# Normalising the first five tiles of a graph layer in one batch, with the input and the first weights on one DMA queue

## The chip, the cores and the metric

The kernel runs on one core of one Trainium2 chip. The metric is the device time of one execution in microseconds (us), as the median of several runs. Five engines work side by side, each in the order of its own instruction list: TensorE (PE, with its weight loads listed as PEld), VectorE (DVE), ScalarE (ACT), GpSimd (POOL) and SyncE (SP). SP, ACT and POOL also issue DMAs, each on a queue of its own. Engines wait for each other by semaphores.

## The reference

One layer of a graph transformer on 3125 nodes with 256 channels and 53125 edges sorted by target:

```python
xn = _layernorm(x, axis=-1)
x = x + _L0_gnn_ref(xn, src, dst, edge_weight, gnn_W, gnn_b) + _L0_mix_ref(xn[None], ...)[0]
x = x + _L0_ffn_ref(_layernorm(x, axis=-1)[None], gate_w, gate_b, w1, w2, w3)[0]

def _L0_gnn_ref(x, edge_row, edge_col, edge_val, W, b):
    msgs = edge_val[:, None] * x[edge_col]
    agg = jax.ops.segment_sum(msgs, edge_row, num_segments=N_NODES)
    return jnp.einsum('nf,of->no', agg, W) + b
```

`_L0_mix_ref` is a linear attention with 8 heads: keys and queries pass elu + 1, and the sum over all nodes of K^T V is needed before any output. Two layer norms and a two-layer network follow. `_L0_ffn_ref` is a mixture of 16 experts with two chosen for each node. Everything that this text is about happens before the sum K^T V is complete.

## The kernel before

The 3125 nodes are held as 25 tiles of 125 rows, in `x_all` (partition, tile, channel). The opening loops over the tiles, `for t in range(NT)`, and does three things for each:

- `normed(t)`: DVE writes `xn = (x - mean) * rstd` (line 417), PE turns it with two transposes into `tok` (L429), ACT copies it to `xnT` (L430). Tile t + 1 is normed before tile t is projected.
- `projected(t)`: PE multiplies by the three joined weights `wcat`: node transform and keys into `big` (L438), values into `tok` (L440). ACT makes `ek` and `k_sb` (L442, L444), the copy `y` (L449) and `v_sb` (L448). DVE joins `ek` and `k_sb` to the key (L446). SP stores `y` (L450), after which it may issue a later load (`load_later`: the x tiles 15 to 19 after tile 0, 20 to 24 after tile 1).
- `summed(t - 1)`: PE adds K^T V of the tile before to `pkv` (L462). It reads `k_sb`, so it waits for the DVE step of L446. PE's list in the opening is thus tok(t+1), big(t), values(t), pkv(t-1), over and over.

The mean and the variance of a tile come from `bn_stats` (L104) and `bn_aggr` (L105) on DVE. The reciprocal square root is worked out on DVE, for a batch of tiles at once, by `rsqrt` (L92 to L99): four small instructions and three rounds of three, 13 in all, each of which needs the one before. `BATCHES` says which tiles share one such chain, and `AHEAD` after which `normed(t)` the moments of which tiles are taken. `factors` (L391, L392) adds two small instructions for each batch.

```python
LOADS = ((0, 2), (2, 5), (5, 10), (10, 15), (15, 20), (20, 25))
BATCHES = ((0, 2), (2, 5), (5, 12), (12, 25))
AHEAD = {1: (2, 5), 2: (5, 9), 3: (9, 12), 4: (12, 15), 6: (15, 17), 9: (17, 21), 10: (21, 25)}
```

`LOADS` says in which pieces x is loaded. The first two pieces are issued at once on SP's queue, the third and fourth when the moments of the first batch have been found.

Beside this, `windows()` prepares the edges, in pieces that are called by `LISTS` after certain tiles. DVE makes `heads` from the first target of each row of edges, PE turns it into a row (`ph`, L244) after a run of matmuls on ones, `busy(16)` (L240), which do no useful work. DVE counts with `cmp_h` (L249) and a reduction (L251), and gets five columns `row_i` (L254). POOL gathers `rows` with them by five indirect DMAs (L258). For each of these, DVE compares (`cmp_r`, L268), reduces (L269) and works out `start_i` (L270 to L273), with which POOL gathers `win` (L274). From `win` DVE makes keys (L287 to L302), after which PE, ACT and POOL build `keys` and `wgts`. They are needed from tile 18 (`HOT`), where the adjacency matrices begin (L336 to L360).

The instructions of each engine are put in order by a scheduler when the kernel is built: pieces of different chains lie between each other on DVE, and each engine keeps that order strictly.

Of the kernel before, what the change touches and what calls it, by code (L numbers as in the profile page):

```python
# [18 lines left out]
C = 256  # L19
# [31 lines left out]
ATT_EPS = 1e-6  # L51
LN_EPS = 1e-5
LOADS = ((0, 2), (2, 5), (5, 10), (10, 15), (15, 20), (20, 25))
BATCHES = ((0, 2), (2, 5), (5, 12), (12, 25))

LISTS = {1: 1, 6: 1, 7: 2, 8: 2, 14: 1, 15: 1, 16: 1}
AHEAD = {1: (2, 5), 2: (5, 9), 3: (9, 12), 4: (12, 15), 6: (15, 17), 9: (17, 21), 10: (21, 25)}
HOT = 18
GROUP = 4

# [2 lines left out]
def tile_gps_layer(ctx: ExitStack, tc: tile.TileContext, a: dict, out: bass.AP):  # L63
    nc = tc.nc
# [37 lines left out]
    def stats(mv, src):  # L102
        st = small.tile([P, 6], F32, name="bn_st")[: src.shape[0]]
        nc.vector.bn_stats(st, src)  # L104
        return nc.vector.bn_aggr(mv, st)  # L105
# [55 lines left out]
    def load_x(queue, t0, t1):  # L161
        return queue.dma_start(x_all[:, t0:t1, :], a["x"][:, t0:t1, :])

    wcat = w_mix.tile([128, 2, 3 * C], F32, name="wcat")
    load_x(nc.sync, *LOADS[0])
    nc.scalar.dma_start(dst_0, a["dst"].rearrange("(p j) -> p j", p=V)[:, 0:1])
    for i, name in enumerate(("gnn_WT", "Wk", "Wv")):
        nc.scalar.dma_start(wcat[:, :, i * C : (i + 1) * C], a[name].rearrange("(k p) o -> p k o", p=128))
    load_x(nc.sync, *LOADS[1])
    wq = w_mix.tile([128, 2, C], F32, name="wq")  # L170
    wm = w_mix.tile([128, 2, C], F32, name="wm")
    w1 = w_mix.tile([128, 4, F], F32, name="w1")
# [47 lines left out]
    def bank_a(of=4 * P):  # L220
        return adj_ps.tile([128, 512], F32, name="pa")[:, :of].rearrange("p (i e) -> p i e", e=of // 4)
# [8 lines left out]
    def windows():  # L230
# [6 lines left out]
        def busy(n):  # L237
            pd = bank_a()
            for i in range(n):
                nc.tensor.matmul(pd[:, i % 4, :], lhsT=ones, rhs=ones, start=True, stop=True)  # L240

        busy(16)
        ph = bank_a()[:V, 0, :V]
        nc.tensor.matmul(ph, lhsT=ones[:V, :V], rhs=heads, start=True, stop=True)  # L244
        yield ins
# [148 lines left out]
    def moments(t0, t1):  # L394

        for i in range(t0, t1):
            found = stats(mv[:, i, :], x_all[:, i, :])
        for t0, end in BATCHES:
            if end == t1:
                ready[t0] = rsqrt(mv[:, t0:t1, 1], t1 - t0)  # L400
        return found

    pieces = windows()
    with tc.issue_after(next(pieces).ins):
        found = moments(*BATCHES[0])

# [3 lines left out]
    def normed(t):  # L410

        nonlocal rstd, r0
        for t0, t1 in BATCHES:
            if t == t0:
# [4 lines left out]
        with tc.issue_after(ins.ins):  # L419
            for batch in BATCHES:  # L420
                if t == batch[0]:
                    factors(*batch, rstd)
            for _ in range(LISTS.get(t, 0)):
                next(pieces, None)
            if t in AHEAD:
                moments(*AHEAD[t])
        ptr = a_ps.tile([128, 2, P], F32, name="tok", bufs=3)
# [259 lines left out]
    for g, (nt, n_adj, n_early) in enumerate(groups):  # L687
# [5 lines left out]
        i = 0  # L693
# [599 lines left out]
```

## Time and profile before

| | |
|---|---|
| median of 3 runs | 1035.18 us (1035.09 to 1035.54) |
| the profiled execution: its time, its span | 1034.76 us, 1033.0 us |
| PE busy | 1004.1 us, 97% of the span |
| DVE busy | 654.8 us, 63% |
| ACT, POOL busy | 263.1 us, 215.7 us |
| mean granted TensorE clock | 0.997 |
| DVE busy in 5 to 10, 10 to 15, 15 to 20, 20 to 25, 25 to 30 us | 4.48, 4.75, 5.00, 4.59, 5.00 us of 5 each |

The times in the profile count from the start of the span. A row of the timeline has the start, the time from the first start to the last end, the engine, the line of the kernel, the operation, the tiles that it writes and reads, and how many instructions are merged; in brackets stands the idle time before it and what ended it. A float32 matmul is listed as two records of PE.

### The profile page before, as it was taken

The numbers are of one execution on the slowest core, as the hardware profiler recorded it, in microseconds if no ns is written. First come the engines' busy times: TensorE is split into PE (matmuls) and PEld (weight loads), VectorE is DVE, ScalarE is ACT, GpSimd is POOL, SyncE is SP. The second block draws the span as 40 slices with busy tenths as digits, with TensorE's granted clock in tenths as the row PEclk, the third lists the DMA queues.
The fourth block names the chain that finished last, engine by engine and source line by source line (L and its number), as shares of the span: only waits on it lengthen the run. The fifth ranks groups of instructions, "written<-read, shape, count | busy, mean of one in ns | idle before, by whom it ended". The sixth has DMA issues, their size and how long they took to land.

```text
span 1033.0 us, 16284 instructions
## 1 busy us (share of the span) xinstructions
PE 1004.1 (97%) x6006; PEld 804.3 (78%) x6006; DVE 654.8 (63%) x1750; ACT 263.1 (25%) x577; POOL 215.7 (21%) x200
## 2 busy tenths in 40 slices
PE   8999999999999999999999999999999999999995
PEld 5667666686786877878877888887888888888884
DVE  8878699889887897956598148786932222222221
ACT  3666423323223133222131000003111111111110
POOL 3420101023100000000000001114535444545432
PEclk9999999999999999999999999999999999999998
DMA  6444104344343444544454446565757757667662
GB/s 216 93 135 140 52 34 174 127 135 138 124 137 137 140 159 142 179 164 143 153 184 155 154 159 172 184 193 180 225 141 222 244 173 228 201 201 226 205 191 26
DMA packets 70024, 165.01 MB, mean 160 GB/s; under 512 B 10816, under 2 KB 29584, under 8 KB 65964
## 3 DMA queue, kind: packets, MB, share of 16 engines
q1 hardware_dynamic: 53466, 138.02, 39.3%
q0 software_dynamic: 15520, 25.04, 10.7%
q8 instruction: 50, 0.82, 0.3%
q10 hardware_dynamic: 946, 0.79, 0.2%
q14 instruction: 42, 0.34, 0.1%
HBM read 105.85 MB, written 57.93 MB: 159 GB/s over the span
## 4 chain that ended last, share of the span: by engine, by line
PE 70%; DVE 11%; issue 2%; ACT 0%; POOL 0%; POOLq 0%; ACTq 0%; DVEq 0%
PE ph L1002 17%; PE pb L626 13%; PE po L1028 10%; PE po L739 8%; PE pa L356 6%; PE big L663 5%; PE tok L674 3%; DVE wone L341 2%; PE pa L626 1%; PE ptr L988 1%; PE big L478 1%; DVE one L336 1%; DVE wone L351 1%; PE ph L800 1%; PE big L490 1%
## 5 line engine op out<-in xcount | busy, mean ns | idle before, releaser
L1002 PE MATMUL ph<-xTb,wt 128*128 128x256 f32 (+2 forms) x992 | 204.5, 355 | 0.8 <-issue 0.8
L1002 PEld LDWEIGHTS ph<-xTb,wt 128*128 128x128 f32 x992 | 171.5, 190 | 24.8 <-ACT xTb L991 4.7
L626 PE MATMUL pb<-y_early,nbr 125*125 125x256 f32 x736 | 170.6, 382 | 0.4 <-DVE x_all L628 0.4
L341 DVE TENSOR_TENSOR wone<-one,wgts 128x1536 bf16<-128x1536 bf16 x150 | 141.1, 953 | 25.5 <-PE pa L356 25.3
L626 PEld LDWEIGHTS pb<-y_early,nbr 125*125 125x125 f32 x736 | 133.7, 188 | 18.6 <-DVE x_all L628 1.0
L356 PEld LDWEIGHTS <-one 128*128 128x128 bf16 x1875 | 117.3, 97 | 39.1 <-issue 18.8
L359 ACT COPY adj<-pa 128x512 f32<-128x512 f32 (+1 forms) x157 | 91.8, 586 | 195.5 <-PE pa L356 169.4
L356 PE MATMUL pa<-wone,one 128*128 128x128 bf16 x1875 | 130.5, 219 | 2.1 <-DVE wone L341 0.9
L1009 DVE TENSOR_TENSOR hid<-hid,ph 128x512 f32<-128x512 f32 (+2 forms) x62 | 38.3, 618 | 145.7 <-PE ph L1002 136.9
L1028 PE MATMUL po<-wt,hid 128*128 128x256 f32 (+1 forms) x456 | 115.2, 385 | 0.8 <-DVE yb L1031 0.7
L739 PE MATMUL po<-y_late,nbr 125*125 125x256 f32 x450 | 102.3, 381 | 0.5 <-DVE x_all L628 0.5
L336 DVE TENSOR_TENSOR one<-iota,keys 128x1024 bf16<-128x1024 bf16 x150 | 101.1, 695 | 0.6 <-POOL wgts L318 0.6
L1032 POOL DMA_INDIRECT out<-yb,to_l x45 | 70.9, 1576 | 114.6 <-DMA out<-yb,to_l 51.0
L1028 PEld LDWEIGHTS po<-wt,hid 128*128 128x128 f32 (+1 forms) x456 | 79.2, 184 | 17.6 <-DVE yb L1031 5.6
L739 PEld LDWEIGHTS po<-y_late,nbr 125*125 125x125 f32 x450 | 82.4, 188 | 12.1 <-DVE x_all L628 0.9
L1008 ACT ACTIVATE hid<-ph 128x512 f32<-128x512 f32 (+2 forms) x62 | 33.6, 542 | 208.5 <-PE ph L1002 202.5
L1031 DVE TENSOR_SCALAR yb<-po,sh 128x256 f32<-128x256 f32 (+1 forms) x57 | 27.5, 482 | 57.3 <-PE po L1028 55.2
L752 POOL IOTA rev<- 125x16 f32 x1 | 0.2, 154 | 295.4 <-PE pb L626 295.4
L701 POOL TENSOR_TENSOR x_all<-x_all,cb 128x256 f32<-128x256 f32 x25 | 25.7, 1050 | 147.0 <-DVE x_all L628 139.4
L628 DVE TENSOR_TENSOR x_all<-x_all,pb 125x512 f32<-125x512 f32 (+1 forms) x37 | 24.3, 658 | 41.7 <-PE pb L626 41.7
L663 PE MATMUL big<-xnT,w 128*128 128x500 f32 (+1 forms) x112 | 48.8, 548 | 0.0
L674 PE MATMUL tok<-w,hT 128*125 128x256 f32 x200 | 47.9, 383 | 0.0
(285 smaller groups left out, 1197.8 us busy)
## 6 DMA issues: line engine op xcount, KB each, us to landing
wt<-in_w SPq DMA_DIRECT2D x28, 1536.0 KB
adj_d<-adj SPq DMA_DIRECT2D x156, 256.0 KB
nbr<-adj_d SPq DMA_DIRECT2D x25, 576.0 KB
nbr<-adj_d SPq DMA_DIRECT2D x50, 256.0 KB
nbr<-adj_d SPq DMA_DIRECT2D x25, 512.0 KB
wt<-in_w POOLq DMA_DIRECT2D x3, 1536.0 KB
out<-x_all SPq DMA_DIRECT2D x25, 125.0 KB
x_all<-in_x SPq DMA_DIRECT2D x4, 640.0 KB
```

The costliest lines, as they stand in the source:

```text
L336: nc.vector.tensor_tensor(one.rearrange("p b h e j -> p (b h) e j"), iota_2[:, None, :, :].to_broadcast(shape), ql.rearrange("p b h j -> p ...
L341: nc.vector.tensor_tensor(wone, one[:, :, 1:2, :, :].to_broadcast(shape), w[:, :, :, None, :].to_broadcast(shape), op=ALU.mult)
L356: nc.tensor.matmul(pa[:, j, :], lhsT=one[:, j // 2, 0, :, j % 2], rhs=wone[:, j // 2, i, :, j % 2], start=(i == 0), stop=(i == 2))
L359: copied = nc.scalar.copy(rows[:, :n, :], pa[:, :n, :])
L626: nc.tensor.matmul(pb[:V, i, :], lhsT=rows[:V, k - t0, :V], rhs=y_of(k)[:V], start=(k == t0 and i == 0), stop=(k == t1 - 1), skip_group_ch ...
L663: nc.tensor.matmul(ph[:, :w], lhsT=w1[:, k, j * 128 : (j + 1) * 128], rhs=rhs, start=(k == 0), stop=(k == 3))
L674: nc.tensor.matmul(po, lhsT=hT[:, j, i * V : (i + 1) * V], rhs=w2[:, j, :], start=(j == 0), stop=(j == 3))
L739: last = nc.tensor.matmul(pg, lhsT=rows[:V, k - t0, :V], rhs=y_of(k)[:V], start=(k == t0), stop=(k == t1 - 1))
L1002: last = nc.tensor.matmul(p[:, m, :w], lhsT=self.wt[:, i, k * F + at : k * F + at + 128], rhs=self.xT[:, k, :w], start=(k == 0), stop=(k = ...
L1009: self.units = nc.vector.tensor_tensor(hid, hid, pre[1], op=ALU.mult)
L1028: last = nc.tensor.matmul(po[:n_r, r, :], lhsT=self.hid[:, k, r * LANES : r * LANES + n_r], rhs=self.wt[:, 2, k * C : (k + 1) * C], start= ...
L1032: made.append(nc.gpsimd.indirect_dma_start(out=out[:, :], out_offset=bass.IndirectOffsetOnAxis(ap=at, axis=0), in_=yb[:n_r, r, :], in_offs ...
```

## The change

Four things are changed. The first batch has five tiles in place of two, so that the batches are 5, 4, 6 and 10 tiles in place of 2, 3, 7 and 13. The later moments are taken in other portions and after other tiles. The three pieces of `wcat` are issued on SP's queue behind both first pieces of x, where they were issued on ACT's queue. And `busy(16)` becomes `busy(24)`.

```diff
-BATCHES = ((0, 2), (2, 5), (5, 12), (12, 25))
+BATCHES = ((0, 5), (5, 9), (9, 15), (15, 25))
...
-AHEAD = {1: (2, 5), 2: (5, 9), 3: (9, 12), 4: (12, 15), 6: (15, 17), 9: (17, 21), 10: (21, 25)}
+AHEAD = {2: (5, 7), 3: (7, 9), 4: (9, 12), 5: (12, 15), 9: (15, 18), 10: (18, 21), 11: (21, 25)}
...
     load_x(nc.sync, *LOADS[0])
     nc.scalar.dma_start(dst_0, a["dst"].rearrange("(p j) -> p j", p=V)[:, 0:1])
+    load_x(nc.sync, *LOADS[1])
     for i, name in enumerate(("gnn_WT", "Wk", "Wv")):
-        nc.scalar.dma_start(wcat[:, :, i * C : (i + 1) * C], a[name].rearrange("(k p) o -> p k o", p=128))
-    load_x(nc.sync, *LOADS[1])
+        nc.sync.dma_start(wcat[:, :, i * C : (i + 1) * C], a[name].rearrange("(k p) o -> p k o", p=128))
...
-        busy(16)
+        busy(24)
```

The order of the instructions, as built: PE's is the same but for the eight more matmuls, POOL's is the same, ACT loses its three DMA issues, SP gains them behind the second piece of x and has the small store `first_d` (L283) two stores of `y` earlier. On DVE the order differs in the first 180 or so of some 1,870 rows, up to the keys of the edges, and is the same from there to the end.

## The prediction

> **What bounds the kernel now.** First the engines' busy time in the page: PE is busy nearly all the time, so the end is set by PE's idle time and by useless work on it.
>
> ```profile
> PE 1004.1 (97%) x6006; PEld 804.3 (78%) x6006; DVE 654.8 (63%) x1750; ACT 263.1 (25%) x577; POOL 215.7 (21%) x200
> ```
>
> Then the waits of PE in the first 140 us (waiting tile and line, what released it, us in total, times, longest):
>
> ```profile
> PE tok L429 <- DVE less L392: 2.6, 1, 2.6
> PE pa L240 <- POOL ones L134: 1.9, 1, 1.9
> PE tok L429 <- DVE xn L417: 0.4, 1, 0.4
> PE pkv L462 <- DVE k_sb L446: 0.3, 1, 0.3
> ```
>
> The largest wait is one of 2.6 us for a normed tile. The timeline of the opening shows where it comes from (start, time taken, engine, line):
>
> ```profile
> 4.11 0.74 DVE L104 BATCH_NORM_STATS2 bn_st<-x_all 128x6 f32<-128x256 f32 x2
> ...
> 5.11 0.17 DVE L92 TENSOR_SCALAR rs_v<-mv 128x2 f32<-128x2 f32 x1
> ...
> 7.55 0.41 DVE L417 TENSOR_SCALAR xn<-x_all,mv,rs_y 128x256 f32<-128x256 f32 x1
> ...
> 8.34 0.74 DVE L104 BATCH_NORM_STATS2 bn_st<-x_all 128x6 f32<-128x256 f32 x2
> ...
> 9.73 0.17 DVE L92 TENSOR_SCALAR rs_v<-mv 128x3 f32<-128x3 f32 x1
> ...
> 12.18 0.17 DVE L254 CAST row_i<-row_f 125x5 int32<-125x5 f32 x1
> ...
> 12.69 1.41 POOL L258 DMA_INDIRECT rows<-in_dst,row_i  x1 [9.30 <-DVE rs_s L98]
> ...
> 13.50 0.69 DVE L417 TENSOR_SCALAR xn<-x_all,mv,rs_y 128x256 f32<-128x256 f32 x1
> ...
> 14.33 0.41 PE L429 MATMUL tok<-ident,xn 125*128 125x125 f32 x2 [2.58 <-DVE less L392]
> ...
> 15.38 0.38 DVE L446 SCALAR_TENSOR_TENSOR k_sb<-ek,k_sb 125x256 f32<-125x256 f32 x1
> ```
>
> The first chain runs from 4.11 to 7.55. The second, for tiles 2 to 4, starts only then, is mixed with the edges' counting, and gives xn at 13.50. PE, done with tiles 0 and 1 at 11.76, waits to 14.33. From there PE's own steps set the pace, 3.24 us a tile:
>
> ```profile
> 17.16 0.61 PE L462 MATMUL pkv<-v_sb,k_sb 125*128 125x129 f32 x4
> 20.40 0.61 PE L462 MATMUL pkv<-v_sb,k_sb 125*128 125x129 f32 x4
> ...
> 26.89 0.61 PE L462 MATMUL pkv<-v_sb,k_sb 125*128 125x129 f32 x4
> ...
> 47.23 0.68 PE L462 MATMUL pkv<-v_sb,k_sb 125*128 125x129 f32 x4 [0.32 <-DVE k_sb L446]
> ...
> 60.59 0.61 PE L462 MATMUL pkv<-v_sb,k_sb 125*128 125x129 f32 x4
> ```
>
> These are pkv(0), (1), (3), (9) and (13). I use them as posts: whatever the change does has happened by pkv(13), since from there on all five engines have their old order and edge work follows PE. From 26.89 to 60.59 are 33.70 us, where ten steps take 32.43: small waits for L446 cost 1.27 us there. DVE, 63% busy on average, is 90 to 100% busy from 5 to 30 us.
>
> **The first chain** grows by three tiles. Two take 1.00 us from 4.11 to 5.11, three take 1.39 from 8.34 to 9.73: 0.39 a tile, 1.17 in all. The 13 steps of rsqrt stay 2.44 us (5.11 to 7.55), and a five-column operand in place of two costs nothing (0.17 us with 2 and with 13 columns). So xn(0) starts at 8.72, and PE, 0.47 us behind as before, turns it at 9.19, not at 8.02. The batches are four before and after, so no chain is saved in number.
>
> **busy(24)** adds 16 records. The run's records come about 0.21 us apart at first, 0.11 at its end (32 take 5.3 us in all; 11 touch the last full microsecond, 7 the second). At 0.11 it ends 1.8 us later, near 8.9, and `ph` before 9.2: hidden, by xn(0). Without that cover it would cost 1.8 us, at 0.21 3.4. [...]
>
> **One queue.** x and `wcat` ahead of tile 0 are 0.66 + 0.79 MB. Even at the 190 GB/s of the first 5 us, from a start near 2.0, all has landed by 9.6; at the 308 GB/s of the next 5 us, before 7. The first `big` needs it at 10.1 (8.91 + 1.17). I take nothing, and at most 0.3 for the third x piece, which is issued 1.2 us later. SP waits nowhere else for the change; `first_d` sits two stores of y earlier, and nobody in the opening waits for a y store.
>
> **The wait removed** is 2.58. If only PE counted, pkv(0) would move from 17.16 to 15.76 (+1.17 - 2.58 = -1.40). But pkv(0) reads k_sb(0), and in the changed order DVE does all of this from xn(0) to L446 of tile 0: five xn, seven stats with their aggregates, cmp_h, the reduction, row_i and 12 of the 13 steps of the second rsqrt. Against the list before (7.83 us, from 7.55 to 15.38) that is two xn more (0.33 each), one stats (0.33) and two aggregates (0.085 each), less two of by/less (0.07) and one step (0.19): +0.83. L446 then starts at 8.72 + 8.66 = 17.4. Adding up the new list by its steps from start to start, with six steps of rsqrt hidden, gives 16.8. I take 17.1. With its 0.40 and 0.15 to PE, pkv(0) comes at 17.65: **+0.5** (0.2 to 0.8). PE's wait of 2.58 becomes one of 1.9 in front of pkv(0).
>
> **Tiles 1 to 3.** row_i falls 5.6 to 5.9 us behind xn(0), at 14.3 to 14.6, not 12.18, and the first gather is issued 0.5 later: 14.9, not 12.69. Up to 17.8 gathers moved 0.30 MB, and one is 0.21 MB, so the first landed near 17.5, 4.8 after its issue; it will land at 19.7 or later. In the changed order the first cmp_r stands ahead of k_sb(1), where before two more k_sb were ahead of it. With 20.2 for the landing k_sb(1) starts at 20.75: pkv(1) at 21.3, **+0.9**. Between k_sb(1) and k_sb(3) DVE has four cmp_r (0.51), three reductions (0.50), two xn and two k_sb (0.33 each) and 22 small ones (0.07 to 0.08 hidden): 6.6 to 6.9. Beside them POOL's gathers stretch an instruction now and then: xn took 0.69 during the first gather, 0.41 otherwise. I add 0.3. k_sb(3) starts at 27.8 and pkv(3) at 28.35, **+1.5** (0.6 to 2.5).
>
> [...]
>
> **What comes back.** Before, the cmp_r work and the late `win` gathers pressed on k_sb(4) to k_sb(11), which is the 1.27. In the changed order the last start_i stands ahead of k_sb(4), near 30 in place of 32.85, so `win` lands earlier and DVE is ahead from there. I take 1.1 of it back. Sum: +1.5 - 1.1 = **+0.4**. The profiled time of 1034.76 becomes 1035.2; the median lies 0.42 above the profiled one, so 1035.6. Bounds: -0.65 with pkv(3) at 27.5 and all 1.27 back; +2.0 with pkv(3) at 28.9 to 29.4 and only half of it back. With 0.3 for a median's spread that is 1034.2 to 1037.3.
>
> **Rivals.** (a) DVE keeps up, and PE alone counts: -1.4, and -2.7 if the 1.27 goes as well. For it: the wait of 2.58 is real and PE has nothing else to wait for. Against: DVE's list ahead of L446, which would have to be 1.9 us shorter.
> (b) The first gather lands late. At 20.6 to 22.0 the gathers moved 0.04 MB beside 0.37 MB of an x load: the load held the fourth up by some 1.4 us. Now that load comes up to 1.4 us earlier and the gathers 2.2 later, so it may meet the first. Each us past 20.2 moves k_sb(1) by one and isn't given back: at 21.9 the whole is +2.1, at 22.5 +2.7. Against: the first gathers came through beside the load before it.
> (c) The waits only change names, and the total is within 0.2 us: the forecast's lower half.
>
> **How the numbers follow.** 0.2% is 2.07 us, about what a measurement of this kernel can tell from no change. Forecast with (c), 0.72: within it but for 0.03 slower. (a), 0.14: within it at -1.4, and 0.04 below it. (b), 0.14: 0.10 slower, the rest within. So faster 0.04, same 0.83, slower 0.13.
>
> **What would show it.** Right: no wait of tok L429 near 12, a wait of 1.5 to 2.5 us of pkv L462 on k_sb, xn(0) at 8.7, pkv(0) at 17.4 to 18.0, pkv(3) late by 1 to 2 us, pkv(9) no longer waiting, pkv(13) near 61.0. Wrong: pkv(0) before 16.5 (rival a), pkv(1) past 22.5 (b), `big` waiting for `wcat`, or a difference that arises after 61 us.

## The result, and the profile after

The changed kernel takes 1038.05 us in the median of ten runs (1037.22 to 1039.52), the kernel before 1035.14 (ten runs). The ratio is 1.0027 (95% interval 1.0018 to 1.0036): slower by 2.9 us. The forecast was 1035.6, with a range to 1037.3. The profiled execution took 1038.04 us, its span is 1036.3 us, 3.3 more than before.

The busy line of the page hardly differs: PE has 16 more records.

```profile
PE 1007.6 (97%) x6022; PEld 807.2 (78%) x6022; DVE 652.5 (63%) x1750; ACT 263.4 (25%) x577; POOL 216.4 (21%) x200
```

The waits of PE in the first 140 us of the changed kernel (waiting tile and line, releaser, us in total, times, longest):

```profile
PE pkv L462 <- DVE rs_v L92: 1.9, 1, 1.9
...
PE pkv L462 <- DVE rs_y L99: 0.7, 1, 0.7
```

The wait of `tok` (L429) is gone, and two waits of `pkv` stand in its place. The releaser's name is that of the DVE instruction nearest in time: `pkv` reads `k_sb`, which DVE ends just then. The timeline of the changed kernel shows the opening:

```profile
4.24 0.75 DVE L104 BATCH_NORM_STATS2 bn_st<-x_all 128x6 f32<-128x256 f32 x2
...
6.41 0.17 DVE L92 TENSOR_SCALAR rs_v<-mv 128x5 f32<-128x5 f32 x1
...
8.91 0.41 DVE L417 TENSOR_SCALAR xn<-x_all,mv,rs_y 128x256 f32<-128x256 f32 x1
...
9.66 0.38 PE L244 MATMUL pa<-heads,ones 125*125 125x125 f32 x2
...
11.88 0.78 DVE L249 TENSOR_TENSOR cmp_h<-pa,thr 125x625 f32<-125x625 f32 x1
...
14.28 0.17 DVE L254 CAST row_i<-row_f 125x5 int32<-125x5 f32 x1
...
14.78 1.41 POOL L258 DMA_INDIRECT rows<-in_dst,row_i  x1 [11.39 <-DVE rs_y L95]
...
16.50 1.23 POOL L258 DMA_INDIRECT rows<-in_dst,row_i  x1 [0.31 <-issue]
...
16.80 0.33 SPq L162 DMA_DIRECT2D x_all<-in_x  x1
...
21.36 0.61 DVE L268 TENSOR_TENSOR cmp_r<-rows,thr 125x425 bf16<-125x425 int32 x1 [1.89 <-DMA rows<-in_dst,row_i]
21.88 0.42 DVE L446 SCALAR_TENSOR_TENSOR k_sb<-ek,k_sb 125x256 f32<-125x256 f32 x1
...
22.45 0.68 PE L462 MATMUL pkv<-v_sb,k_sb 125*128 125x129 f32 x4 [1.87 <-DVE rs_v L92]
...
25.39 0.61 DVE L268 TENSOR_TENSOR cmp_r<-rows,thr 125x425 bf16<-125x425 int32 x1 [1.84 <-DMA rows<-in_dst,row_i]
...
27.14 0.42 DVE L446 SCALAR_TENSOR_TENSOR k_sb<-ek,k_sb 125x256 f32<-125x256 f32 x1
...
27.70 0.68 PE L462 MATMUL pkv<-v_sb,k_sb 125*128 125x129 f32 x4
```

The five-tile chain ends at 8.91. The edges' counting is done at 14.28, not 12.18, so the gathers are issued 2.1 us later (14.78, before 12.69). The load of x tiles 15 to 19 also comes later (14.05, before 12.25), that of tiles 20 to 24 1.0 earlier (16.80, before 17.77), so both loads now lie closer together and beside the first gathers. DVE then stands still twice, 1.89 and 1.84 us, for `rows` from the first and the second gather. In the built order each of these two compares is ahead of a `k_sb`, and `pkv` starts 0.57 us behind the start of that. Tile by tile:

| start of | pkv(0) | pkv(1) | pkv(2) | pkv(3) | pkv(9) | pkv(13) |
|---|---|---|---|---|---|---|
| before | 17.16 | 20.40 | 23.64 | 26.89 | 47.23 | 60.59 |
| after | 17.10 | 22.45 | 27.70 | 31.29 | 50.82 | 63.79 |
| difference | -0.06 | +2.05 | +4.06 | +4.40 | +3.59 | +3.20 |

The loss arises between pkv(0) and pkv(3); 1.20 us of it comes back by pkv(13), and +3.20 there is nearly the +3.3 of the span.

### The profile page after: what moved, and what is told of

The parts are those of the page before. It is cut to its first block, busy times and chain, and to the rows that moved or that the text cites. A ratio compares the mean times of both kernels' runs of the same rounds, so it can differ in the third digit from the quotient of the medians.

```text
span 1036.3 us, 16316 instructions
## 1 busy us (share of the span) xinstructions
PE 1007.6 (97%) x6022; PEld 807.2 (78%) x6022; DVE 652.5 (63%) x1750; ACT 263.4 (25%) x577; POOL 216.4 (21%) x200
## 4 chain that ended last, share of the span: by engine, by line
PE 70%; DVE 11%; issue 2%; ACT 0%; POOL 0%; POOLq 0%; ACTq 0%; DVEq 0%
PE ph L1002 17%; PE pb L626 13%; PE po L1028 9%; PE po L739 8%; PE pa L356 6%; PE big L663 5%; PE tok L674 3%; DVE wone L341 2%; PE pa L626 1%; PE ptr L988 1%; PE big L478 1%; DVE one L336 1%; DVE wone L351 1%; PE ph L800 1%; PE big L490 1%
## 5 line engine op out<-in xcount | busy, mean ns | idle before, releaser
L341 DVE TENSOR_TENSOR wone<-one,wgts 128x1536 bf16<-128x1536 bf16 x150 | 140.8, 950 | 25.6 <-PE pa L356 25.4
L438 PE MATMUL big<-wcat,xnT 128*125 128x512 f32 x100 | 48.7, 608 | 0.2 <-ACT xnT L430 0.2
```

The costliest lines, as they stand in the source:

```text
L341: nc.vector.tensor_tensor(wone, one[:, :, 1:2, :, :].to_broadcast(shape), w[:, :, :, None, :].to_broadcast(shape), op=ALU.mult)
L438: nc.tensor.matmul(pyk, lhsT=xnT[:, k, cols], rhs=wcat[:, k, : 2 * C], start=(k == 0), stop=(k == 1))
```

## The experiments

Three sets were run, each on another chip and beside its own runs of the kernel before (medians 1038.0, 1034.65 and 1035.38 us). So ratios are compared, and times only inside a set. Edits are against the changed kernel unless it is said otherwise.

Two theories stood at the start. One: the gathers land late, because they meet the load of x tiles 20 to 24, and DVE waits for them ahead of `k_sb`. The other came from the clock in the changed kernel, by the windows (columns: busy time and count of PE, PEld, DVE, ACT, POOL; then granted clock, DMA share, GB/s):

```profile
24.00:26.00 2.00, 2.00 (x4) 0.73 (x3) 0.61 (x3) 0.00 (x0) 0.00 (x0) 0.50 0.58 157
```

Behind the wait of 1.87 PE ran at half clock, so the loss could be the clock's.

**e1: the later pieces of the edges come two tiles later.**

```diff
-LISTS = {1: 1, 6: 1, 7: 2, 8: 2, 14: 1, 15: 1, 16: 1}
+LISTS = {1: 1, 8: 1, 9: 2, 10: 2, 14: 1, 15: 1, 16: 1}
```

> The changed kernel with the work on the gathered rows (compare, reduce, start_i) called two tiles later: LISTS has 8:1, 9:2, 10:2 in place of 6:1, 7:2, 8:2. In DVE's order the first compare now stands behind k_sb(2), the second ahead of k_sb(3). Theory 1 (pkv(1) and pkv(2) wait for k_sb, and k_sb waits on DVE behind a compare whose gather has not landed): the waits of 1.9 us on DVE go, pkv(0) stays at 17.1, pkv(1) comes at 20.3 and pkv(2) at 23.6, pkv(13) near 59.5 in place of 63.8; the median is 1033.9 to 1034.6, less than the 1035.1 of before. Theory 2 (the half clock between 23.9 and 27.2 us is what costs): the same direction, since no idle time is left to bring the clock down, but only some 1.9 us are won, 1036.1. Theory 3 (the queue or the longer busy run costs): no change, 1038.

Measured: 1038.54 us, ratio 1.0007 (0.9998 to 1.0016). The scheduler now puts k_sb(1) and k_sb(2), at 20.03 and 22.73, ahead of the first compare, at 23.38. The early waits vanish: pkv(1), (2), (3) start at 20.59, 23.91 and 27.15. But `win` is gathered later, and the waits of PE in this run show a new one, at pkv(9):

```profile
PE pkv L462 <- DVE k_sb L446: 1.8, 1, 1.8
```

With 0.53 at pkv(10) it brings pkv(13) to 62.61. So it is the place of the compares in DVE's order that makes the late gathers cost something, and to move them only shifts the price.

**e2: PE is kept busy.** In front of pkv(0), (1) and (2) stand 3, 8 and 8 useless matmuls on ones.

```diff
+        if t in (1, 2, 3):
+            pd = bank_a()
+            with tc.issue_after(last.ins):
+                for i in range((3, 8, 8)[t - 1]):
+                    last = nc.tensor.matmul(pd[:, i % 4, :], lhsT=ones, rhs=ones, start=True, stop=True)
```

> The changed kernel with useless matmuls on ones put on PE just ahead of pkv(0), pkv(1) and pkv(2): 3, 8 and 8 of them, about as long as the waits there (0.7, 1.8 and 1.8 us at full clock). They do not touch DVE's work, but keep PE busy, so that the clock is not halved. Theory 1 (k_sb waits behind the gathers): pkv(1) stays near 22.5 and pkv(2) near 27.7, though the clock is full between 24 and 27 us; the median stays within 0.5 us of 1038.0. Theory 2 (the half clock costs 1.94 us, the sum by which the records of 23.18 to 27.70 are longer than at full clock): pkv(2) comes 1.9 us earlier and the median falls to 1036.1.

Measured: 1040.08 us, ratio 1.0020 (1.0011 to 1.0028). The clock reads 1.00 in every window from 20 to 28 us, and pkv(1) and pkv(2) still come at 23.19 and 29.02, because DVE's compares come at 22.11 and 26.19, behind waits of 2.60 and 1.41 for `rows`. DVE's order isn't quite that of the changed kernel (one more reduction stands ahead of k_sb(2)), so the posts can't be compared to the tenth. But a full clock gains nothing here, and the second theory falls; e5 bears this out.

**e3: the load of x tiles 20 to 24 goes behind tile 5.**

```diff
-        if t in (0, 1):
-            load_x(nc.sync, *LOADS[4 + t])
+        if t in (0, 5):
+            load_x(nc.sync, *LOADS[4 + t // 5])
```

> The changed kernel with the load of x tiles 20 to 24 issued after tile 5 in place of tile 1, so that it is out of the way of the gathers. DVE's order up to k_sb(3) is the same. If that load holds the gathers up (the forecast's rival b): the first compare starts at 20 or so in place of 21.36, the second at 22 to 23 in place of 25.39, pkv(3) comes 1.5 to 2.5 us earlier and the median falls to 1035.5 to 1036.5. If the gathers are slow by themselves: the compares start when they did, and the median stays at 1038.0 within 0.4.

Measured: 1046.05 us, ratio 1.0078 (1.0065 to 1.0091). As a time it says nothing on the question, since the load, issued at 34.3, now comes too late, by the timeline of this run:

```profile
47.92 0.75 DVE L104 BATCH_NORM_STATS2 bn_st<-x_all 128x6 f32<-128x256 f32 x2 [10.40 <-DMA x_all<-in_x]
```

The first 30 us do answer, by the same timeline:

```profile
21.61 0.68 DVE L268 TENSOR_TENSOR cmp_r<-rows,thr 125x425 bf16<-125x425 int32 x1 [1.52 <-DMA rows<-in_dst,row_i]
...
23.78 0.59 DVE L268 TENSOR_TENSOR cmp_r<-rows,thr 125x425 bf16<-125x425 int32 x1
```

The first compare still waits, to 21.61, 6.23 us behind its gather's issue at 15.38 (6.58 in the changed kernel). The second, at 23.78, finds its rows: at most 6.69 behind the issue at 17.09, where the changed kernel has 8.89. From pkv(1) to pkv(2) are 3.32 us, not 5.25. So without the load of tiles 20 to 24 the second gather is 2.2 us faster or more. For the first gather this run shows nothing: 6.23 lies too near to the 6.48 to 7.30 us that it takes in the four executions with both loads at their places (the changed kernel, e2, e5, e8), and the load of tiles 15 to 19 left 1.6 us ahead of it, not 0.7 as in the changed kernel.

**e4: only the queue and `busy(24)` stay;** `BATCHES` and `AHEAD` are those of before.

```diff
-BATCHES = ((0, 5), (5, 9), (9, 15), (15, 25))
+BATCHES = ((0, 2), (2, 5), (5, 12), (12, 25))
...
-AHEAD = {2: (5, 7), 3: (7, 9), 4: (9, 12), 5: (12, 15), 9: (15, 18), 10: (18, 21), 11: (21, 25)}
+AHEAD = {1: (2, 5), 2: (5, 9), 3: (9, 12), 4: (12, 15), 6: (15, 17), 9: (17, 21), 10: (21, 25)}
```

> The changed kernel with BATCHES and AHEAD of before: only the queue of the weights and busy(24) are left of the change. In DVE's order k_sb(1) stands ahead of the first compare again, k_sb(2) behind it. Theory 1: no compare waits for a gather long enough to hold k_sb up by more than 0.5 us; PE waits near 13 us for the normed tile 2 again; median 1035.1 to 1036.0. Theory 3 (the queue or the busy run costs): 1037 or more.

Measured: 1038.96 us, ratio 1.0010 (1.0000 to 1.0020). Even without the long chain the edges come late: `ph` at 9.74, `cmp_h` at 12.75 (before 10.29), the first gather at 15.54. PE waits 1.52 at pkv(0) and 1.26 at pkv(2); the wait for the normed tile 2 doesn't come back. `cmp_h` doesn't wait for `ph`, which ends 2.6 us before it: in the built order it stands behind the whole chain of the second batch, where before it lay within that chain. The first compare waits 0.92 for its rows here too. So more useless matmuls seem to have a price, through the order in which the edges' work is put; as a time the loss is at the edge of what the set can tell.

The second set has the changed kernel again as its control, and three edits.

**e5: the changed kernel once more.**

> The changed kernel once more, as the control for the three that run beside it. Slower than before by 2 to 3.5 us. If its profile shows pkv(1) at 22 to 23 and pkv(2) near 27.7 with the first compare at 21.4 and the second at 25.4, both within 0.7 us, the gathers' landing is the same from one execution to the next.

Measured: 1037.19 us, ratio 1.0028 (1.0016 to 1.0040). By its timeline DVE again waits for the same two gathers, and pkv(2) comes at 27.83:

```profile
21.39 0.61 DVE L268 TENSOR_TENSOR cmp_r<-rows,thr 125x425 bf16<-125x425 int32 x1 [1.77 <-DMA rows<-in_dst,row_i]
...
25.52 0.60 DVE L268 TENSOR_TENSOR cmp_r<-rows,thr 125x425 bf16<-125x425 int32 x1 [1.96 <-DMA rows<-in_dst,row_i]
...
27.83 0.68 PE L462 MATMUL pkv<-v_sb,k_sb 125*128 125x129 f32 x4 [1.88 <-DVE start_f L270]
```

Its windows give the clock, in the first of the last three columns:

```profile
24.00:26.00 2.00, 1.95 (x7) 0.94 (x5) 0.48 (x1) 0.88 (x4) 0.00 (x0) 1.00 0.71 155
26.00:28.00 2.00, 0.17 (x1) 0.20 (x2) 2.00 (x10) 0.85 (x3) 1.21 (x1) 1.00 0.42 138
```

In this execution the clock stayed at 1.00, and PE stood idle for 1.88 us before pkv(2); in the first it ran at half clock and had no idle time there. Both start pkv(2) 0.14 us behind the end of k_sb(2), which is at 27.56 in the first and at 27.69 here. The half clock only filled a wait.

**e6: x tiles 15 to 24 are loaded early,** right behind tiles 5 to 14, and not after the first stores.

```diff
-        if t in (0, 1):
-            load_x(nc.sync, *LOADS[4 + t])
...
-    for batch in LOADS[2:4]:
+    for batch in LOADS[2:]:
```

> The changed kernel with the loads of x tiles 15 to 24 issued right behind those of tiles 5 to 14, not after the projections of tiles 0 and 1: they should be over by 16 or 17 us, before the gathers move data. DVE's order is the same as in the changed kernel. If those loads hold the gathers up: the first compare starts at 19.5 to 20.5 in place of 21.4, the second at 21 to 23 in place of 25.4, pkv(2) comes 2 to 3.5 us earlier, pkv(3) 1.5 to 3, and the median falls by 1.5 to 3 us against the control. If the gathers are slow by themselves: compares and median as in the control.

Measured: 1034.92 us, ratio 1.0004 (0.9995 to 1.0013), 2.3 us below the control. DVE's order is the same as in the changed kernel, and the gathers are issued at the same times, 14.79 and 16.51. The DMA view of the changed kernel from 14 to 26 us (queue, packets, MB, share of 16 engines; then issues) has the loads beside the gathers:

```profile
q1 hardware_dynamic: 578, 1.60, 46.1%
q0 software_dynamic: 733, 0.99, 35.7%
...
x_all<-in_x SPq DMA_DIRECT2D x2, 640.0 KB
```

That of e6 in the same window has only the stores of y there:

```profile
q0 software_dynamic: 897, 1.08, 38.9%
q1 hardware_dynamic: 429, 0.49, 11.8%
```

The first two compares start 6.48 and 8.89 us behind the issue of their gathers in e5, both after a wait, and 5.71 and 6.16 in e6, where only the first waits; by e6's DMA view the median of its five gathers, from issue to landing, is 5.7. The timeline of e6, whose line numbers are two lower, has the first wait for `rows` shorter and the second gone (the fifth compare, at 27.44, now waits 0.45):

```profile
20.50 0.60 DVE L266 TENSOR_TENSOR cmp_r<-rows,thr 125x425 bf16<-125x425 int32 x1 [1.01 <-DMA rows<-in_dst,row_i]
...
21.58 0.68 PE L460 MATMUL pkv<-v_sb,k_sb 125*128 125x129 f32 x4 [0.99 <-DVE rs_v L92]
...
22.67 0.59 DVE L266 TENSOR_TENSOR cmp_r<-rows,thr 125x425 bf16<-125x425 int32 x1
...
24.96 0.69 PE L460 MATMUL pkv<-v_sb,k_sb 125*128 125x129 f32 x4
...
29.10 0.68 PE L460 MATMUL pkv<-v_sb,k_sb 125*128 125x129 f32 x4 [0.66 <-DVE start_f L268]
```

pkv(13) comes at 61.60, against 63.92 in the control: -2.32, as much as the medians differ (-2.27). This settles the main cause: with `busy(24)` in place, 2.3 of the loss of 2.5 us in this set go when the two x loads are not beside the gathers. Which of the two loads holds up which gather e6 doesn't tell; e3 does for the second.

**e7: the useless matmuls are 16 again.**

```diff
-        busy(24)
+        busy(16)
```

> The changed kernel with busy(16) in place of busy(24). The scheduler then puts the counting of the edges ahead of the moments of tiles 5 to 8 on DVE, and the first compare behind k_sb(1). Theory 1: the gathers are issued about 1 us earlier (13.8 or so), only k_sb(2) and k_sb(3) stand behind a compare, PE's wait ahead of pkv(1) goes and pkv(2) waits by 0.5 to 2 us; the median is 1.5 to 2.5 us below the control. If the order on DVE does not matter: median as in the control, as PE's busy run is hidden by the first chain in either.

Measured: 1035.94 us, ratio 1.0016 (1.0006 to 1.0025), with a wide spread (1033.2 to 1039.07). `ph` comes at 7.06, the scheduler puts `cmp_h` (10.27) and row_i (12.82) ahead of the moments of tiles 5 to 8, the first gather is issued at 13.31, and pkv(0) and pkv(1) come at 15.67 and 18.91, earlier than before the change. But the gathers are slower still: the first is awaited to 21.47, 8.16 us behind its issue, and the second, issued at 15.03, is awaited to 24.54, 9.5 us later:

```profile
24.54 0.60 DVE L268 TENSOR_TENSOR cmp_r<-rows,thr 125x425 bf16<-125x425 int32 x1 [1.35 <-DMA rows<-in_dst,row_i]
...
25.62 1.20 PE L462 MATMUL pkv<-v_sb,k_sb 125*128 125x129 f32 x4 [3.31 <-DVE start_f L270]
...
27.04 2.85 PE L438 MATMUL big<-wcat,xnT 128*125 128x512 f32 x4
...
30.59 0.61 PE L462 MATMUL pkv<-v_sb,k_sb 125*128 125x129 f32 x4
```

Its windows have the clock at half behind that wait:

```profile
26.00:28.00 2.00, 2.00 (x8) 1.48 (x8) 2.00 (x14) 0.37 (x1) 1.25 (x1) 0.50 0.32 102
```

Here the half clock does cost: from pkv(2) to pkv(3) are 4.97 us where the pace is 3.24, and PE waited for nothing between.

**e8: `wcat` on ACT's queue again.**

```diff
-        nc.sync.dma_start(wcat[:, :, i * C : (i + 1) * C], a[name].rearrange("(k p) o -> p k o", p=128))
+        nc.scalar.dma_start(wcat[:, :, i * C : (i + 1) * C], a[name].rearrange("(k p) o -> p k o", p=128))
```

> The changed kernel with the three pieces of the first weights back on ACT's queue. DVE's order is that of the changed kernel. Theory 1: the queue is no part of the loss, median within 0.4 us of the control, first compare within 0.4 us of the control's. Theory 3 (the queue costs, by a later x or a later dst): xn(0) 0.3 us or more earlier than the control's 8.9, and the median lower by that.

Measured: 1037.97 us, ratio 1.0041 (1.0028 to 1.0054). xn(0) starts at 9.21, against 8.95 in the control, because the third tile's moments wait 0.18 for x and the rest follows 0.26 later; pkv(13) comes at 64.14 against 63.92. The one queue thus costs nothing and seems worth 0.2 to 0.3 us, by the posts of one execution each; the intervals overlap, so the times don't show it.

The third set puts the two causes together.

**e9: e6 and `busy(16)`** (both edits as above).

> The changed kernel with both cures: the loads of x tiles 15 to 24 right behind those of 5 to 14, and busy(16). With busy(16) alone pkv(1) came at 18.9 without a wait and pkv(2) waited 3.3 us for k_sb(2) behind the second compare at 24.6. Theory (an x load in the way of the gathers holds the compares up): the second compare starts at 20.5 to 21.5, pkv(2) comes at 22.2 to 23, the clock is not halved, and the next limit is the win gathers ahead of pkv(9): pkv(13) at 58 to 59.5. The median is 1 to 2.5 us below before. If the gathers stay late in this order: pkv(2) at 25 or so, and the median 0 to 1.5 us above before.

Measured: 1033.35 us, ratio 0.9981 (0.9972 to 0.9990): faster than before. The first gather is issued at 13.38, the compares at 20.05 and 21.85 wait for no DMA, pkv(1), (2), (3) come at 19.07, 22.92 and 26.24, with one wait of 0.37, and pkv(13) at 58.73. By its timeline:

```profile
20.05 0.57 DVE L266 TENSOR_TENSOR cmp_r<-rows,thr 125x425 bf16<-125x425 int32 x1
...
21.85 0.59 DVE L266 TENSOR_TENSOR cmp_r<-rows,thr 125x425 bf16<-125x425 int32 x1
...
22.92 0.68 PE L460 MATMUL pkv<-v_sb,k_sb 125*128 125x129 f32 x4 [0.37 <-DVE start_f L268]
```

With e5, e6 and e7 this gives a square:

| ratio to before | `busy(24)` | `busy(16)` |
|---|---|---|
| x tiles 15 to 24 loaded after stores | 1.0028 | 1.0016 |
| loaded early | 1.0004 | 0.9981 (third set) |

**e10: the kernel before with the early loads** (the edit of e6 on the kernel before).

> The kernel before with only the loads of x tiles 15 to 24 moved up to those of 5 to 14. There no compare waits for a gather, and PE's wait of 2.6 us for tile 2 is set by DVE's chains, so the theory says: within 1 us of before, and the wait stays. If moving those loads is worth something by itself (a full queue later on): 1 us or more faster.

Measured: 1035.44 us, ratio 1.0000 (0.9991 to 1.0009). Without the new batches the early loads gain nothing; the wait of 2.58 for `tok` stays.

**e11: e9 with the edges' pieces one tile later.**

```diff
-LISTS = {1: 1, 6: 1, 7: 2, 8: 2, 14: 1, 15: 1, 16: 1}
+LISTS = {1: 1, 7: 1, 8: 2, 9: 2, 14: 1, 15: 1, 16: 1}
```

> As the run with early x and busy(16), with the work on the gathered rows called one tile later (LISTS 7:1, 8:2, 9:2). k_sb(2) then stands ahead of the second compare. If a compare still holds up k_sb in the run without this: 0.3 to 1 us faster than that. If the win gathers ahead of pkv(9) are the limit by then: slower by 0.5 to 1.5 us than that, as they start later.

Measured: 1034.63 us, ratio 0.9995 (0.9985 to 1.0004). The early pace holds (pkv(2) at 22.40), but waits of 0.82 and 0.54 appear at pkv(9) and (10) behind `win`, as in e1; pkv(13) comes at 60.56.

**e12: e6 and `busy(14)`.**

```diff
-        busy(24)
+        busy(14)
```

> As the run with early x and busy(16), with busy(14), which the scheduler answers with k_sb(2) ahead of the second compare while LISTS stays. PE's useless run ends 1.5 us ahead of xn(0) or more, so it costs nothing, but PE idles longer there and the clock may be lower in some executions. Expected the same as with busy(16) within 0.7 us; the posts from pkv(3) tell which order is the better.

Measured: 1032.69 us, ratio 0.9973 (0.9964 to 0.9983), the lowest of all; its interval overlaps that of e9, so 14 against 16 isn't told apart. The first compare comes at 20.02 and the second, behind k_sb(2), at 22.23; neither waits. By its timeline PE keeps its pace of 3.24 us:

```profile
17.54 0.61 PE L460 MATMUL pkv<-v_sb,k_sb 125*128 125x129 f32 x4
...
20.78 0.61 PE L460 MATMUL pkv<-v_sb,k_sb 125*128 125x129 f32 x4
...
24.02 0.61 PE L460 MATMUL pkv<-v_sb,k_sb 125*128 125x129 f32 x4
...
27.27 0.61 PE L460 MATMUL pkv<-v_sb,k_sb 125*128 125x129 f32 x4
```

This profiled execution was the slowest of its runs (1034.04), with a clock of 0.63 and 0.52 from 10 to 14 us. It beats the kernel before with the changed batches and the one queue kept, so those were not what lost the time.

## Why the prediction was wrong

**The first chain: right.** xn(0) came at 8.91 for a forecast of 8.72: 0.13 of it is the later start (4.24, not 4.11), 0.06 the chain.

**busy(24): right for PE, wrong for DVE's order.** It ran on to `ph` at 9.66; the forecast had it before 9.2. In other runs with 24, `ph` came from 8.78 (e3) to 10.25 (e2). PE's time was indeed covered by xn(0) and by the wait at pkv(0). But `ph` is what `cmp_h` reads, and the place of `cmp_h` in DVE's order, settled when the kernel is built, changes with it. DVE never waits for `ph` in these traces: in the changed kernel `ph` ends at 10.04 and `cmp_h` starts at 11.88, in its turn. So the late gathers there come from the order, not from the length of this execution's busy run. In e7 the counting moves ahead of the moments and the gathers are issued 1.6 us earlier than in the control (13.31, not 14.91). With the loads out of the way, 16 in place of 24 are worth 0.23% (e9 against e6, in two sets). In e9 PE no longer waits at pkv(0), which comes 1.37 us earlier (15.74, not 17.11), so there a shorter busy run may count as well; the two weren't separated.

**One queue: right,** and on the good side (e8).

**The wait removed: right in kind, 0.55 too dear.** pkv(0) came at 17.10, not 17.65, since DVE's list from xn(0) to k_sb(0) took 7.56 us (8.91 to 16.47) and not 8.38. PE's wait there was 0.74, not 1.9: DVE came 0.55 sooner, and PE, which turned tile 0 at 9.88 and not at 9.19, about 0.6 later. (At 11.76, in the kernel before, PE had turned tiles 0 and 1 but projected only tile 0; no sum uses this.)

**Tiles 1 to 3: the step that failed.** The issue of the first gather was right (14.78 for 14.9). Its landing was taken at 20.2; the compare started at 21.36, 1.16 later. For the second gather no wait was in the sum at all; it was 1.84. The two make 3.00, and pkv(3) missed its forecast by 2.90 (+4.40, not +1.5). The forecast had worked out the four compares and reductions behind k_sb(1) as DVE's work, as if their rows were there. That work it had right, with some luck: from k_sb(1) to k_sb(3) DVE took 8.85 us (21.88 to 30.73), 7.01 without the wait, for 7.05 in the forecast (20.75 to 27.8), but the terms as listed there add up to 6.4 to 6.6, not 6.6 to 6.9. Of the first landing, 0.4 is the gather's own: with no load beside it it took 5.7 us (e6), for 5.3 in the forecast (14.9 to 20.2).

**What comes back: right.** 1.20 of the 1.27 for a forecast of 1.1, and pkv(9) no longer waits.

**The sum as a whole.** With the x loads out of the way (e6) the kernel lies 0.04% above the kernel before, which is the forecast's +0.4 us: the sum describes a kernel whose gathers meet no load. Part of that is luck, as pkv(3) is at 29.10 there, not 28.35, and pkv(13) at 61.60, not 61.0. The range's upper end is 0.2 short of its own terms (+2.0, 0.42 and 0.3 on 1034.76 make 1037.5); the measured 1038.05 lies above either.

**The rivals.** Rival (b) names the mechanism, and it got 0.14. The argument against it, that the first gathers came through beside the load before, could not be read from the kernel before: there the first compare starts 10.48 us behind its gather's issue (23.17, 12.69) for other reasons, so a late landing would not have shown. And its price reached only to the first gather: at a landing of 21.36 it would have given 0.4 + 1.16 = +1.6, half the loss. The sign to look for, pkv(1) past 22.5, was missed by 0.05 (22.45), as the larger part of the miss came one tile later.

The runs show the direction: the second gather takes 8.89 us beside the loads, at most 6.16 without (e6). How a load on SP's queue holds up a gather on POOL's, no run here shows.

## What to carry to other kernels

When a chain in front of a gather grows, ask which bulk load will be under way at the gather's new time, and price every gather that an engine in strict order waits for, not the first one alone. Try to issue a load that nobody needs soon ahead of gathers that an engine will wait for: here that turned a loss of 0.28% into none that can be told (e6), and the same batches into a gain of 0.2 to 0.3% once the useless matmuls were few again (e9, e12). In the kernel before, where nothing waited for the gathers, it gained nothing (e10). Work that is "hidden" on its own engine can still delay another engine's chain through what it stands in front of (DVE's waits of 1.77 and 1.96 us ahead of `k_sb` became waits of 1.76 and 1.88 of PE, e5), and can change the order that a scheduler builds (with `busy(24)` the gathers were issued 1.6 us later than with `busy(16)`, e5 and e7).

## What the runs showed of the hardware

**The clock after idle time differs between executions.** In the kernel before PE stood idle for 2.58 us and the clock stayed at 1.00; in e10, which differs only in when x is loaded, it stood idle for the same 2.58 us and ran at half clock afterwards. The windows of the kernel before, then those of e10:

```profile
16.00:18.00 2.00, 2.00 (x13) 1.65 (x12) 2.00 (x10) 1.50 (x5) 1.70 (x2) 1.00 0.61 175
```

```profile
16.00:18.00 2.00, 2.00 (x5) 1.13 (x4) 2.00 (x10) 0.74 (x3) 1.70 (x2) 0.50 0.50 141
```

pkv(0) came there at 18.72, not 17.16, and pkv(13) 0.46 later than in the kernel before. The changed kernel itself shows both: half clock behind a wait of 1.87 us in its first execution, 1.00 behind waits of 1.76 and 1.88 in e5. In four executions the clock stayed halved for some 3.4 us. In the changed kernel, by windows of 0.2 us, it is 0.50 from 23.9 to 27.1 us, 0.89 in the window before that and 0.58 in the one behind. For the others the stretch is an estimate from the means of windows of 2 us, with 0.50 as the lower value: from 15.6 to 19.1 us in e10 (0.91, 0.50 and 0.73 from 14 to 20), from 25.6 to 29.0 in e7 (0.89, 0.50 and 0.75 from 24 to 30) and from 10.5 to 13.9 in e12 (0.63 and 0.52 from 10 to 14). What decides whether the clock falls behind such a wait, no run here shows.

A wait of 2.58 us thus cost more in one execution than in another (in e10, at half clock behind it, pkv(0) came 1.56 us later than in the kernel before), and the half clock cost nothing where another wait would have followed (pkv(2) at 27.70 in the changed kernel, at 27.83 at full clock in e5). Whether it is the clock that spreads e7's runs over 5.9 us no run shows.

**One load took long beside smaller transfers.** The 640 KB of x that e3 issued at 34.3 were there at 47.9, 13.6 us later. Beside it, from 34 to 48 us, POOL's queue moved 0.78 MB, of which three loads of 128 KB and some small ones are 0.42 (an estimate from their sizes; the rest should be of the last gathers of `win`), and SP's queue had the stores of y; which of them held it up wasn't separated.
